# Two transposes of a graph kernel moved from TensorE to VectorE, with their inputs fetched in blocks

## The chip, the cores and the metric

The kernel runs on one core of one Trainium2 chip. A core has five engines that run their own instruction streams in order: TensorE (PE in the profile; PEld is its weight load), VectorE (DVE), ScalarE (ACT), GpSimd (POOL) and SyncE (SP), which here only issues DMAs. Engines wait for each other, and for DMAs, on semaphores. The metric is the device time of one launch in microseconds.

## What is computed

64 graphs, each with 256 nodes and 256 features, in float32. Layer 0 is a normalised graph convolution with residual and layer norm, layer 1 a long convolution over nodes and a message pass, whose results go through a GRU cell, again with residual and layer norm.

```python
# layer 0
deg = adjacency_matrix.sum(axis=-1)
deg = jnp.where(deg != 0, deg, 1.0)
d_inv_sqrt = deg ** (-0.5)
norm_adj = d_inv_sqrt[:, :, None] * adjacency_matrix * d_inv_sqrt[:, None, :]
a_plus = norm_adj + alpha_eff * jnp.eye(N, dtype=adjacency_matrix.dtype)
h = jnp.einsum('bnm,bmf->bnf', a_plus, x)
x = _layernorm(x + jnp.einsum('bnf,pf->bnp', h, W) + b, axis=-1)
# layer 1
xc = jnp.transpose(x, (0, 2, 1))
h = jax.nn.relu(_bn(_conv1d(xc, conv1_w, 0), ...))
h = _bn(_conv1d(h, conv2_w, 8), ...)                 # 17 taps
x_conv = jnp.transpose(jax.nn.relu(h + xc), (0, 2, 1))
s = x @ w_se.T + b_se
dist = sq[:, :, None] + sq[:, None, :] - 2.0 * jnp.einsum('bnd,bmd->bnm', s, s)
A = jnp.exp(-dist) * mask                            # mask is adj
msg = jax.nn.relu(x @ w_msg.T + b_msg)
x_nmp = jnp.einsum('bnm,bmd->bnd', A, msg)
x_in = jnp.concatenate([x_conv, x_nmp], axis=-1)
# GRU cell of (x_in, x), then residual and layer norm
x = _layernorm(x + gru(x_in, x), axis=-1)
```

## The kernel before

[...] the kernel needs adj and the layer 0 result x1 in two layouts: as they lie in memory (nodes on partitions) and transposed.

**Stages.** The 64 graphs are split into four parts q of 16. The convolution with 17 taps is done in the frequency domain, over a whole part at a time. First comes a setup stage (about 30 to 300 us): graphs 0 to 15 go through layers 0 and 1, and beside them `weights()` turns the taps into frequency weights (p_u on TensorE, copies u_set on ScalarE, a VectorE and a GpSimd pass, and three stores of 480 KB a part to the DRAM tensor ud, issued by GpSimd). Then, for each part q: the frequency products of that part (p_k, twelve steps, loading ud again), their inverse, and the GRU gates (p_rz and p_n) of its 16 graphs, with the two layers of the next 16 graphs beside them. The last part has no following graphs.

**One graph.** `layer0(g)` (lines 337 to 411): loads adj_t and x_t (L99, L101; two buffers each, issued by SP three graphs ahead); degrees on ScalarE by an accumulating copy whose main output goes to a part of adjT that is written later (L347); dis = deg^-0.5 on GpSimd (L360); four TensorE transposes of adj into a PSUM bank (L369) and a ScalarE copy into adjT (L370); the diagonal on VectorE (L372); x scaled by dis into x1 on ScalarE (L382); x_t + b on GpSimd (L383). It then yields. The second piece is p_hT (L390) and its ScalarE copy hT (L395), the third p_out (L400), the residual on VectorE (L405), the layer norm (VectorE L311 to L313 and L322, GpSimd L314, ScalarE L324) and the store of x1 to DRAM (L410), issued from ScalarE's queue. x1 has two buffers.

`x1_transposed(g)` (L413 to L420) is four TensorE transposes of x1 (L419) and a ScalarE copy (L420) into xn, the transposed input of layer 1.

`layer1(g)` (L422 to L510): p_conv (L434), bias on VectorE (L437) and relu on ScalarE (L438) give h; p_msg (L455) gives msg; p_dft (L471) takes h to the frequency domain; p_rows (L484) and p_dist (L495) give the distances, the exponential (L496) and the multiply by adjT (L497) give aT; p_nmp (L504) and its copy (L508) end it, with the store of xn (L509).

**Order.** Each function is a generator. `graphs()` walks over layer1(g) and, after each of its pieces, takes a piece of layer0(g+2) or of the other work, as the tuple PLACES says:

```python
PLACES = (("other",), ("layer0",), (), (), ("layer0",), ("other", "layer0"), ())
```

This is the order in which instructions are recorded. The order on each engine is made from it at build time by a list scheduler, which orders what is ready by estimated times; `tc.issue_after(op)` forces an instruction behind another. At run time each engine follows its list in order, so an instruction that waits holds all those behind it. Tiles come from rotating pools: a tile with `bufs=1` is written again only when all readers of its last content are done, a DMA that stores it among them.

Of the kernel before, what the change touches and what calls it, by code (L numbers as in the profile page):

```python
# [9 lines left out]
F32 = mybir.dt.float32  # L10
# [4 lines left out]
P = 128  # L15
# [11 lines left out]
def kernel(  # L27
# [27 lines left out]
    nc = tc.nc  # L55
# [7 lines left out]

    FL, NT = 48, 32
    GT = N // NT
    Q = P // GT
    NQ = B // Q
    assert N == 256 and D == 256 and B % Q == 0 and TAPS == FL - NT + 1 and FL == 3 * NT // 2
# [23 lines left out]

    xin, ain = {}, {}

    def load(g):
        if g >= B:
            return
        ain[g] = loads.tile([P, NCH, N], F32, name="adj_t")
        nc.sync.dma_start(ain[g], adj[g].rearrange("(c p) m -> p c m", p=P))  # L99
        xin[g] = loads.tile([P, NCH, D], F32, name="x_t")  # L100
        nc.sync.dma_start(xin[g], x[g].rearrange("(c p) f -> p c f", p=P))  # L101

# [9 lines left out]
    vectors = const.tile([16, P], F32, name="bn_in")  # L112
    neg_half = const.tile([P, 4], F32)
    nc.vector.memset(neg_half, -0.5)
    load(0)
    nc.scalar.dma_start(alpha_t, bcast_rows(alpha, 1))

    nc.scalar.copy(bc1[:, :4], neg_half)
    for i, a in enumerate((bn1_g, bn2_g, bn1_b, bn2_b, bn1_m, bn2_m, bn1_v, bn2_v)):
        (nc.sync if i % 2 else nc.scalar).dma_start(vectors[2 * i : 2 * i + 2], a.rearrange("(c p) -> c p", p=P))  # L120
    nc.scalar.dma_start(w0, w0T.rearrange("(k p) o -> p k o", p=P))
    load(1)
    nc.sync.dma_start(b0_t, bcast_rows(b0, D))
    nc.sync.dma_start(wc1[:, :, :D], conv1T.rearrange("(k p) o -> p k o", p=P))
    nc.sync.dma_start(wc1[:, :, D:], w_seT.rearrange("(k p) o -> p k o", p=P))
# [204 lines left out]
    x1_d = [dram.tile([Q, N, D], F32, name=f"x1_d{q}") for q in range(NQ)]  # L330
    xn_d = [dram.tile([P, 2 * DCH, N], F32, name=f"xn_d{g}") for g in range(B)]
    XN = {}
    ALONE = set()
    ADJT, X1, X_SCALED, DIAGONAL = {}, {}, {}, {}


    def layer0(g):

        a_t, x_t = ain.pop(g), xin.pop(g)

        adjT = work.tile([P, NCH, 3, P], F32, name="adjT", bufs=3)
        ADJT[g] = adjT

        deg = small.tile([P, NCH], F32, name="deg")
        def degrees():
            for c in range(NCH):
                nc.scalar.activation(  # L347
                    adjT[:, c, 0:2, :].rearrange("p n q -> p (n q)"), a_t[:, c, :], AF.Copy,
                    accum_out=deg[:, c : c + 1],
                )  # L350

        if g == 1:

            with tc.issue_after(X_SCALED[0]):
                degrees()
        else:
            degrees()
        nc.vector.scalar_tensor_tensor(deg, deg, 0.0, deg, op0=ALU.is_equal, op1=ALU.add)  # L358
        dis = small.tile([P, NCH], F32, name="dis")
        nc.gpsimd.tensor_tensor(dis, deg, neg_half[:, :NCH], op=ALU.pow)  # L360
        adeg = small.tile([P, NCH], F32, name="adeg")
        nc.vector.tensor_scalar(adeg, deg, alpha_t, None, op0=ALU.mult)

        p = bank("p_adjT").rearrange("p (c n) -> p c n", c=NCH)
        for mc in range(NCH):
            for c in range(NCH):
                nc.tensor.transpose(p[:, mc, c * P : (c + 1) * P], a_t[:, c, mc * P : (mc + 1) * P], ident)  # L369
        copied = nc.scalar.copy(adjT[:, :, 0:3:2, :], p.rearrange("p c (n q) -> p c n q", q=P))  # L370
        for mc in range(NCH):
            DIAGONAL[g] = nc.vector.scalar_tensor_tensor(  # L372
                adjT[:, mc, 1, :], ident, adeg[:, mc : mc + 1], adjT[:, mc, 2 * mc, :],
                op0=ALU.mult, op1=ALU.add,
            ).ins


        x1 = work.tile([P, NCH, D], F32, name="x1")
        X1[g] = x1
        with tc.issue_after(copied.ins) if g < 2 else ExitStack():  # L380
            for c in range(NCH):
                X_SCALED[g] = nc.scalar.activation(x1[:, c, :], x_t[:, c, :], AF.Copy, scale=dis[:, c : c + 1]).ins  # L382
        nc.gpsimd.tensor_tensor(x_t, x_t, b0_t.unsqueeze(1).to_broadcast([P, NCH, D]), op=ALU.add)  # L383

        yield
        hT = work.tile([P, DCH, N], F32, name="hT", bufs=1)
        p = bank("p_hT").rearrange("p (k n) -> p k n", k=DCH)
        for k in range(DCH):
            for mc in range(NCH):
                nc.tensor.matmul(  # L390
                    p[:, k, :], x1[:, mc, k * P : (k + 1) * P],
                    adjT[:, mc, 1 - mc : 3 - mc, :].rearrange("p n q -> p (n q)"),
                    start=mc == 0, stop=mc == NCH - 1,
                )
        nc.scalar.copy(hT, p)  # L395
        yield
        p = bank("p_out0").rearrange("p (c o) -> p c o", c=NCH)
        for c in range(NCH):
            for k in range(DCH):
                nc.tensor.matmul(  # L400
                    p[:, c, :], hT[:, k, c * P : (c + 1) * P], w0[:, k, :], start=k == 0, stop=k == DCH - 1
                )
        for c in range(NCH):
            mark(
                nc.vector.scalar_tensor_tensor(  # L405
                    x1[:, c, :], p[:, c, :], dis[:, c : c + 1], x_t[:, c, :], op0=ALU.mult, op1=ALU.add
                )
            )
        layernorm(x1, nc.scalar)
        nc.scalar.dma_start(x1_d[g // Q][g % Q].rearrange("(c p) d -> p c d", p=P), x1)  # L410
        yield

    def x1_transposed(g):  # L413
        x1 = X1.pop(g)
        xn = XN[g] = work.tile([P, 2 * DCH, N], F32, name="xn")
        p = bank("p_x1T").rearrange("p (k n) -> p k n", k=DCH)
        for k in range(DCH):
            for c in range(NCH):
                nc.tensor.transpose(p[:, k, c * P : (c + 1) * P], x1[:, c, k * P : (k + 1) * P], ident)  # L419
        nc.scalar.copy(xn[:, :DCH], p)  # L420

    def layer1(g, place):  # L422
# [3 lines left out]
        xn, adjT = XN.pop(g), ADJT.pop(g)  # L426
        x1T = xn[:, :DCH]
        yield

        h = work.tile([P, NCH, D + NSE], F32, name="h", bufs=1)  # L430
        for c in range(NCH):
# [60 lines left out]
        for c in range(NCH):  # L492
# [2 lines left out]
            nc.tensor.matmul(p, dl[rows, c * P : (c + 1) * P], dr[rows, :], start=True, stop=True)  # L495
            nc.scalar.activation(aT[:, c].rearrange("p n q -> p (n q)"), p, AF.Exp, bias=nsq[:, c : c + 1], scale=2.0)  # L496
        mark(nc.vector.tensor_mul(aT, aT, adjT[:, :, 0:3:2, :]))  # L497
        yield
        if g in ALONE:
            x1_transposed(g + 1)  # L500
        p = bank("p_nmp").rearrange("p (k n) -> p k n", k=DCH)
        for k in range(DCH):
            for mc in range(NCH):
# [418 lines left out]
    def graphs(first, part, others):  # L922


        for i in part:
            load(first + i + 3)
            given = {"layer0": layer0(first + i + 2) if first + i + 2 < B else iter(()), "other": others[i]}
            for piece, _ in enumerate(layer1(first + i, i)):
                yield
                for name in PLACES[piece]:  # L930
                    if next(given[name], "end") != "end":
                        yield
            yield from given["other"]

    with tc.tile_pool(name="setup", bufs=1) as setup:
        load_taps(setup, 0)
# [1 line left out]
        nc.sync.dma_start(bmsg_t, bcast_rows(b_msg, D))  # L938
        firsts = merge(layer0(0), layer0(1))
        run(take(firsts, 2))  # L940
        load(2)
        tables(setup)
        run(firsts)
        scale2 = next(batch_norms(setup))

        def gate_weights():
            for b, half_inputs, cols in ((B11, 0, 0), (T1, 0, 1), (B21, 1, 0), (B22, 1, 1)):
# [71 lines left out]
    for q in range(NQ):  # L1019
        first = (q + 1) * Q  # L1020
        more = q + 1 < NQ
        end = chain(complex_end(q), copies(V2) if more else iter(()))
        if more:
            if q:
                others = [take(late, 3 if i % 3 == 0 else 2) for i in range(AHEAD)]
            else:
                others = [nothing() for _ in range(AHEAD)]
                ALONE.update(range(first, first + AHEAD))
            TILES[0] = V2
            begin = graphs(first, range(AHEAD), others)  # L1030
        sums(0)
        real = real_transform()
        for step in range(STEPS):
            if step < 4:
                run(products(step))
            else:
                run(merge(products(step), take(real, 1)))
                run(complex_begin(step))
            if q:
                run(take(late, (0, 1, 1, 1, 1, 1, 2, 1, 2, 1, 2, 1)[step] if more else step % 2))  # L1040
            else:
                run(take(begin, 3))
        run(real)
        if not q:
            run(paced(begin, end, RATES[q]))
        elif more:
            run(paced(chain(merge(take(late, 20), take(begin, 6), 3), begin), end, RATES[q]))
        else:
            run(paced(late, end, RATES[q]))
            run(end)  # L1050
        if more:
            run(late)
            run(end)
            if q == 0:
                scope.close()
                gate = ctx.enter_context(tc.tile_pool(name="gate", bufs=2))
            early = gates(q, range(EARLY))
            others = [take(early, 5 if q == 0 else 2) for _ in range(Q)]
            run(graphs(first, range(AHEAD, Q), others))
            run(early)  # L1060
            if q == 0:
                scope, AHEAD, V2 = open_ahead(6)
                ctx.enter_context(scope)
            late = gates(q, range(EARLY, Q))
        else:
            run(gates(q, range(Q)))


# [51 lines left out]
```

## Time and profile before

| what | value |
| --- | --- |
| median of 3 runs | 2164.66 us (2161.34 to 2165.57) |
| profiled execution: time, span | 2162.39 us, 2160.6 us |
| granted TensorE clock | 0.993 |
| DMA, mean over the span | 305.65 MB, 251182 packets, 141 GB/s |
| DMA queue of SP's and ScalarE's loads, q1 | 183530 packets, 30.0% of 16 engines |
| DMA queue of stores, q10 | 44480 packets, 8.7% |
| GpSimd's queue, q0 | 23024 packets, 8.5% |
| adj transposes L369 and their copies L370 | 39.8 us on PE, 37.0 us on ACT (64 copies) |
| x1 transposes L419 and their copies L420 | 39.1 us on PE, 37.6 us on ACT (64 copies) |

The durations are those of one profiled execution, whose span is 1.8 us shorter than its device time. Busy times are sums of instruction durations. Matmuls are pipelined, so that a listed TensorE duration may be longer than the time after which the next one starts. A shape is written as partitions x elements per partition. "[1.93 <-DVE ln_mr L322]" after a line of the timeline means that the engine stood idle 1.93 us before it and that VectorE's writing of ln_mr released it.

### The profile page before, as it was taken

Reading aid. Unit: us, or ns where it says so; the run is one execution under the profiler, and the core shown is the slowest. Engines: PE = TensorE matmul, PEld = TensorE weight load, DVE = VectorE, ACT = ScalarE, POOL = GpSimd, SP = SyncE. Lnnn points to the kernel's source line nnn. Section 1 sums busy time; section 2 is a strip of 40 time slices with the busy share of each in tenths; the row PEclk is TensorE's granted clock in tenths of the full one; section 3 lists DMA queues with packets and bytes.
Section 4 is the critical chain, followed back from the end, with each engine's and each line's share of the span. In section 5 each row is a group of like instructions: output and inputs, shape, how many; then the busy total and the mean of one; then the engine's idle time right before and its main releaser. Section 6 shows DMA issues by size and latency. Waiting matters only on the chain.

```text
span 2160.6 us, 29043 instructions
## 1 busy us (share of the span) xinstructions
PE 2058.4 (95%) x9805; PEld 1745.5 (81%) x9805; DVE 1547.2 (72%) x3691; ACT 834.7 (39%) x1857; POOL 665.5 (31%) x640
## 2 busy tenths in 40 slices
PE   7999999887999999899999999999999998999998
PEld 5888788776788888788888888778888887788887
DVE  5555577775568788775556988876556889977776
ACT  4665643456331123455443122446543122222222
POOL 2444310122431244223222133323231124444442
PEclk9999999999999999999999999999999999999999
DMA  4766666434347644243336654325334834444441
GB/s 122 236 193 199 194 197 209 144 123 153 87 123 228 195 110 135 98 132 113 108 94 189 201 165 112 118 99 153 92 97 134 249 113 120 126 123 103 113 107 54
DMA packets 251182, 305.65 MB, mean 141 GB/s; under 512 B 18174, under 2 KB 229714, under 8 KB 251034
## 3 DMA queue, kind: packets, MB, share of 16 engines
q1 hardware_dynamic: 183530, 200.46, 30.0%
q10 hardware_dynamic: 44480, 67.39, 8.7%
q0 software_dynamic: 23024, 35.95, 8.5%
q8 instruction: 78, 1.28, 0.2%
q14 instruction: 70, 0.57, 0.1%
HBM read 200.62 MB, written 103.06 MB: 141 GB/s over the span
## 4 chain that ended last, share of the span: by engine, by line
PE 45%; DVE 13%; issue 8%; POOL 6%; ACT 4%; DMA 1%; ACTq 0%; POOLq 0%; DVEq 0%
PE p_rz L808 17%; PE p_n L845 8%; PE p_k L530 7%; PE p_out L400 2%; PE p_nmp L504 2%; PE p_hT L390 2%; POOL ln_rs L314 1%; PE p_dft L471 1%; PE p_conv L434 1%; POOL xc_g L765 1%; POOL sums L788 1%; POOL sums L787 1%; PE p_msg L455 1%; PE p_dist L495 1%; ACT inputs L778 1%
## 5 line engine op out<-in xcount | busy, mean ns | idle before, releaser
L845 PE MATMUL p_n<-wn,inputs 128*128 128x256 f32 x1536 | 350.0, 381 | 14.8 <-DVE first L821 14.7
L808 PE MATMUL p_rz<-wrz,sums 128*128 128x256 f32 x1536 | 350.9, 381 | 3.3 <-POOL sums L787 2.4
L845 PEld LDWEIGHTS p_n<-wn,inputs 128*128 128x128 f32 x1536 | 285.8, 190 | 59.7 <-DVE first L821 17.9
L808 PEld LDWEIGHTS p_rz<-wrz,sums 128*128 128x128 f32 x1536 | 290.8, 191 | 48.1 <-issue 5.6
L808 PE MATMUL p_rz<-wrz,inputs 128*128 128x256 f32 x1152 | 271.9, 379 | 0.2
L314 POOL TENSOR_TENSOR ln_rs<-ln_rs,neg_half 128x2 f32<-128x2 f32 x129 | 100.5, 779 | 519.3 <-DVE ln_rs L313 448.0
L808 PEld LDWEIGHTS p_rz<-wrz,inputs 128*128 128x128 f32 x1152 | 217.5, 190 | 30.7 <-issue 1.0
L857 ACT ACTIVATE nn<-gn 128x256 f32<-128x256 f32 x128 | 53.2, 416 | 329.8 <-DVE gn L854 329.5
L530 PE MATMUL p_k<-u,VM 128*128 128x256 f32 x736 | 174.5, 380 | 1.6 <-DVE VM L573 0.9
L787 POOL TENSOR_TENSOR sums<-inputs 128x384 f32<-128x384 f32 x64 | 71.1, 1112 | 332.6 <-ACT inputs L778 299.8
L360 POOL TENSOR_TENSOR dis<-deg,neg_half 128x2 f32<-128x2 f32 x64 | 46.0, 718 | 401.6 <-DVE deg L358 389.6
L324 ACT ACTIVATE x_g<-x_g,ln_mr,ln_rs 128x256 f32<-128x256 f32 x128 | 70.0, 593 | 245.9 <-DVE ln_mr L322 245.9
L530 PEld LDWEIGHTS p_k<-u,VM 128*128 128x128 f32 x736 | 138.3, 190 | 22.5 <-DMA u<-ud 2.0
L471 PE MATMUL p_dft<-fwd,h 128*128 128x240 f32 x512 | 119.8, 378 | 27.8 <-ACT h L438 26.7
L390 PE MATMUL p_hT<-adjT,x 128*128 128x256 f32 x512 | 127.9, 392 | 14.4 <-DVE adjT L372 7.7
L471 PEld LDWEIGHTS p_dft<-fwd,h 128*128 128x128 f32 x512 | 95.4, 192 | 48.4 <-ACT h L438 41.6
L434 PE MATMUL p_conv<-wc,xn 128*128 128x259 f32 x512 | 125.8, 388 | 4.9 <-ACT xn L420 4.9
L383 POOL TENSOR_TENSOR x_t<-x_t,b_t 128x512 f32<-128x512 f32 x64 | 86.5, 1352 | 140.6 <-ACT x L382 88.6
L497 DVE TENSOR_TENSOR aT<-aT,adjT 128x512 f32<-128x512 f32 x64 | 44.3, 692 | 113.5 <-ACT aT L496 113.5
L400 PE MATMUL p_out<-w,hT 128*128 128x256 f32 x512 | 123.1, 383 | 1.4 <-ACT hT L395 0.7
L455 PE MATMUL p_msg<-wmsg,xn 128*128 128x256 f32 x512 | 121.5, 380 | 0.0
L504 PE MATMUL p_nmp<-aT,msg 128*128 128x256 f32 x512 | 121.1, 379 | 0.2 <-DVE aT L497 0.2
(154 smaller groups left out, 3898.6 us busy)
## 6 DMA issues: line engine op xcount, KB each, us to landing
u<-ud SPq DMA_DIRECT2D x284, 256.0 KB
xn_d<-xn ACTq DMA_DIRECT2D x64, 512.0 KB
inputs<-xn_d SPq DMA_DIRECT2D x64, 512.0 KB
ud<-u_set POOLq DMA_DIRECT2D x39, 480.0 KB, 6.0
adj_t<-in_adj_dram SPq DMA_DIRECT2D x64, 256.0 KB
x_t<-in_x_dram SPq DMA_DIRECT2D x64, 256.0 KB
x_d<-x ACTq DMA_DIRECT2D x64, 256.0 KB
xc_d<-VM SPq DMA_DIRECT2D x64, 256.0 KB
```

What stands on the lines that cost most here:

```text
L314: nc.gpsimd.tensor_tensor(rs[:, : len(chunks)], rs[:, : len(chunks)], neg_half[:, : len(chunks)], op=ALU.pow)
L383: nc.gpsimd.tensor_tensor(x_t, x_t, b0_t.unsqueeze(1).to_broadcast([P, NCH, D]), op=ALU.add)
L390: nc.tensor.matmul(p[:, k, :], x1[:, mc, k * P : (k + 1) * P], adjT[:, mc, 1 - mc : 3 - mc, :].rearrange("p n q -> p (n q)"), start=mc == ...
L400: nc.tensor.matmul(p[:, c, :], hT[:, k, c * P : (c + 1) * P], w0[:, k, :], start=k == 0, stop=k == DCH - 1)
L434: nc.tensor.matmul(p, x1T[:, k, c * P : (c + 1) * P], wc1[:, k, :], start=k == 0, stop=k == DCH - 1)
L455: nc.tensor.matmul(p[:, c, :], x1T[:, k, c * P : (c + 1) * P], wmsg[:, k, :], start=k == 0, stop=k == DCH - 1)
L471: nc.tensor.matmul(p[:, t0 * FL : t1 * FL], h[:, c, k * P : (k + 1) * P], fwd[:, first : first + t1 - t0, :].rearrange("p t f -> p (t f)") ...
L504: nc.tensor.matmul(p[:, k, :], msg[:, mc, k * P : (k + 1) * P], aT[:, mc].rearrange("p n q -> p (n q)"), start=mc == 0, stop=mc == NCH - 1,)
L530: nc.tensor.matmul(p[:, j * D : (j + 1) * D], v[:, k, :], u[:, k, :], start=k == 0, stop=k == DCH - 1)
L787: nc.gpsimd.tensor_tensor(S[:, 0], A21, A22, op=ALU.add)
L808: nc.tensor.matmul(p[:, j * D : (j + 1) * D], a[:, k], wrz[:, b, k], start=k == 0, stop=k == HALF - 1)
L845: nc.tensor.matmul(p[:, o * D : (o + 1) * D], lhsT, w, start=j == 0, stop=j == len(part) - 1)
```

## The change

VectorE's `transpose` turns each 32x32 block of a tile by itself. To get a full transpose, the blocks must already lie in their transposed places; this is done by the DMA that fetches the tile: `fetch_blocks` reads a 256x256 matrix from DRAM in four transfers of 32 partitions with 16 runs of 32 floats each.

- adj of graphs 2 to 63 is fetched twice: row by row (adj_t, for the degrees) and in blocks (adj_blocks). Both use the two buffers of one tag. VectorE transposes adj_blocks into adjT.
- x1 of graphs 1 to 63 is fetched in blocks from x1_d, to which layer 0 stores it (L410 before, L449 after), and VectorE transposes it into xn. The fetch is recorded after the first piece of layer1(g−1), the transpose right after the multiply of aT and adj in layer1(g−1).
- `behind(op)` puts every later recorded VectorE instruction after the transpose in VectorE's order.
- The first part of layer 0 (degrees, transpose, dis, diagonal) becomes a piece of its own, which `graphs()` runs at the end of the graph before, a graph ahead; the load of adj is issued after the second piece of layer1, that of x in front.
- The x1 tile has one buffer in place of two; x1_blocks has one.
- ALONE, which let some graphs transpose x1 earlier, is gone.

In the changed file the scaling of x is L421, the store of x1 L449, the residual L444, the layer norm's last step L345, the degrees L374, u_set's copy L317, relu of h L487, p_dft L520.

```diff
+    def fetch_blocks(blocks, y):
+        for b in range(NB):
+            nc.sync.dma_start(
+                blocks[b * RB : (b + 1) * RB], y.rearrange("(s r) (k b j) -> b r k s j", r=RB, k=DCH, j=RB)[b]
+            )
+
+    def load_adj(g):
+        if g >= B:
+            return
+        a_t, a_b = loads.tile([P, NCH, N], F32, name="adj_t", tag="adj"), None
+        nc.sync.dma_start(a_t, adj[g].rearrange("(c p) m -> p c m", p=P))
+        if g > 1:
+            a_b = loads.tile([P, DCH, N // RB, RB], F32, name="adj_blocks", tag="adj")
+            fetch_blocks(a_b, adj[g])
+        ain[g] = a_t, a_b
...
+    def behind(op):
+        order.close()
+        order.enter_context(tc.issue_after(op.ins))
...
     def layer0(g):
-        def degrees():
-            for c in range(NCH):
-                nc.scalar.activation(
-                    adjT[:, c, 0:2, :].rearrange("p n q -> p (n q)"), a_t[:, c, :], AF.Copy,
-                    accum_out=deg[:, c : c + 1],
...
+        else:
+            for c in range(NCH):
+                degrees(c, a_t[:, c, :])
+            behind(
+                nc.vector.transpose(
+                    adjT[:, :, 0:3:2, :].rearrange("p k n (s r) -> p k n s r", r=RB),
+                    a_b.rearrange("p k (n s) j -> p k n s j", n=NCH),
                 )
+            )
...
-        p = bank("p_adjT").rearrange("p (c n) -> p c n", c=NCH)
-        for mc in range(NCH):
-            for c in range(NCH):
-                nc.tensor.transpose(p[:, mc, c * P : (c + 1) * P], a_t[:, c, mc * P : (mc + 1) * P], ident)
-        copied = nc.scalar.copy(adjT[:, :, 0:3:2, :], p.rearrange("p c (n q) -> p c n q", q=P))
+        if g < 2:
...
+        if g > 1:
+            yield
+        x_t = xin.pop(g)
-        x1 = work.tile([P, NCH, D], F32, name="x1")
+        x1 = work.tile([P, NCH, D], F32, name="x1", bufs=1, tag="x1" if g else "x1_blocks")
...
+    def fetched(g):
+        XB[g] = work.tile([P, DCH, N // RB, RB], F32, name="x1_blocks", bufs=1)
+        fetch_blocks(XB[g], x1_d[g // Q][g % Q])
+
     def x1_transposed(g):
...
+        if g:
+            behind(nc.vector.transpose(xn[:, :DCH].rearrange("p k (s r) -> p k s r", r=RB), XB.pop(g)))
+            return
...
     def layer1(g, place):
...
         yield
+        if g + 1 < B:
+            fetched(g + 1)
...
         mark(nc.vector.tensor_mul(aT, aT, adjT[:, :, 0:3:2, :]))
-        yield
-        if g in ALONE:
+        if g + 1 < B:
             x1_transposed(g + 1)
+        yield
...
     def graphs(first, part, others):
-            load(first + i + 3)
-            given = {"layer0": layer0(first + i + 2) if first + i + 2 < B else iter(()), "other": others[i]}
-            for piece, _ in enumerate(layer1(first + i, i)):
+            g = first + i
+            load_x(g + 3)
+            given = {"layer0": ZERO.pop(g + 2, iter(())), "other": others[i]}
+            for piece, _ in enumerate(layer1(g, i)):
                 yield
+                if piece == 1:
+                    load_adj(g + 3)
                 for name in PLACES[piece]:
                     if next(given[name], "end") != "end":
                         yield
-            yield from given["other"]
+            if g + 3 < B:
+                ZERO[g + 3] = layer0(g + 3)
+                next(ZERO[g + 3])
+                yield
+            yield from others[i]
```

## The prediction

> **What bounds the kernel now.** I read the engine shares and the chain that ended last first, then the busy time stage by stage, then the order of events inside one graph of the first stage, and last the DMA engines in single microseconds.
>
> The page:
>
> ```profile
> PE 2058.4 (95%) x9805; PEld 1745.5 (81%) x9805; DVE 1547.2 (72%) x3691; ACT 834.7 (39%) x1857; POOL 665.5 (31%) x640
> PE 45%; DVE 13%; issue 8%; POOL 6%; ACT 4%; DMA 1%; ACTq 0%; POOLq 0%; DVEq 0%
> ```
>
> TensorE is the bound over the whole, VectorE second; ScalarE and GpSimd have room. Work taken from TensorE is worth something; work given to VectorE is not free.
>
> Busy time by stretch (length, then PE, PEld, DVE, ACT and POOL busy, granted clock, DMA share, GB/s):
>
> ```profile
> 30.00:252.00 222.00, 217.32 (x1053) 179.27 (x1052) 120.19 (x316) 133.49 (x310) 98.81 (x93) 0.99 0.64 201
> 400.00:526.00 126.00, 104.89 (x500) 83.14 (x498) 91.33 (x289) 74.34 (x166) 26.08 (x26) 0.98 0.37 125
> 912.00:1156.00 244.00, 236.79 (x1153) 198.41 (x1154) 148.27 (x406) 124.01 (x286) 67.36 (x70) 1.00 0.36 109
> ```
>
> By the records of L504 in the same view (8 for each graph), 13 graphs run in the first stretch (setup, with the frequency weights beside them), 7 from 252 to 400, 8 from 400 to 526, 4 to 645, 3+3 at 750–912 and 1262–1427, and 13 each at 912–1156 and 1427–1661 (with gates); none beside the complex products. TensorE is full in the first and third line. In the second it idles 21 us: that stage is a chain of dependences.
>
> What the removed transposes cost (timeline, TensorE):
>
> ```profile
> 1114.44 0.60 PE L419 MATMUL p_x1T<-ident,x 128*128 128x128 f32 x4
> 1114.87 2.76 PE L808 MATMUL p_rz<-wrz,inputs 128*128 128x256 f32 x12
> ```
>
> The next matmuls start 0.43 us later, so four transposes hold TensorE 0.43 us, not the 0.60 listed. In the same way a 256-column matmul record costs 0.216 us (the twelve p_rz records here: next start after 2.59), 1.73 for a group of eight.
>
> One setup graph (timeline, the lines of one layer 0 and one layer 1 picked out):
>
> ```profile
> 111.55 1.89 PE L400 MATMUL p_out<-w,hT 128*128 128x256 f32 x8
> ...
> 118.21 1.09 ACT L324 ACTIVATE x<-x,ln_mr,ln_rs 128x256 f32<-128x256 f32 x2 [1.93 <-DVE ln_mr L322]
> ...
> 119.33 0.37 ACTq L410 DMA_DIRECT2D x_d<-x  x1
> ...
> 120.22 0.63 ACT L438 ACTIVATE h<-h 128x512 f32<-128x512 f32 x1
> ...
> 127.20 1.89 PE L400 MATMUL p_out<-w,hT 128*128 128x256 f32 x8
> ```
>
> The pitch is 127.20−111.55 = 15.65 us. x1 is normalised 7.75 us after p_out (118.21+1.09−111.55), its store to DRAM issued by 119.7 (8.1 us after p_out), and ScalarE goes on at once with relu (L438), which p_dft (L471) waits for, and with the next graph's x scaling (L382), since x1 has two buffers.
>
> When does that store land? The DMA engines from 121 to 122 us and from 124 to 125 (queue: packets, MB, share of 16 engines):
>
> ```profile
> q0 software_dynamic: 82, 0.30, 87.8%
> q10 hardware_dynamic: 28, 0.03, 10.5%
> ...
> q10 hardware_dynamic: 41, 0.04, 10.9%
> ```
>
> Its queue (q10) still moves packets at 125 us, because the 480 KB stores of ud on q0 share the engines: some 5.4 to 5.8 us after issue. In the gates stage the same store, issued at 1142.08, has moved its last packet by about 1145.3, 3.0 to 3.2 us later.
>
> [...]
>
> **The change, part by part.**
>
> TensorE. 62 adj and 63 x1 transposes go: 125 x 0.43 = 54 us, 0.86 us a graph. This is a ceiling, had only where TensorE is the bound.
>
> ScalarE loses 125 copies (578 and 587 ns by their rows), 73 us; it is not the bound.
>
> VectorE gains 125 transposes. The nearest row is L497, an f32 128x512 pass of 692 ns (684 to 694); I take 0.70 us, 125 x 0.70 = 87 us (72% to about 76%). Bounds: 0.55 us (close to ScalarE's 0.59 for such a copy) to 1.4 us (two passes, or blocks written with stride), 69 to 175 us.
>
> DMA. Four transfers per tile, 512 packets of 128 bytes each: 2048 packets. Between 29 and 32 us only small packets move:
>
> ```profile
> q1 hardware_dynamic: 128, 0.01, 3.0%
> ```
>
> 0.030 x 16 x 3 us / 128 = 11 ns each. So 2048 x 11 ns / 16 = 1.4 us of all engines per tile; I take 1.5 to 2, some 3 to 4 us a graph. Upper bound: as long as a 1 KB packet between 122 and 123 us (0.408 x 16 us / 103 = 63 ns), 8 us a tile, which would be more than the setup stage has left (0.36 of 15.65 = 5.6 us). SP gets 500 issues. Row-major adj still comes, for the degrees.
>
> Moved loads. On SP a setup graph now issues four x1 block fetches, adj, four adj block fetches, x_t, then the seven taps loads that p_u needs. The taps thus stand behind x_t's wait for its buffer, which L444 (the old L405) frees about 3 us after p_out; p_u's five come over 7 us after p_out, so I cost this at nothing; uncovered it would be up to 3 us in those graphs. VectorE's x1 transpose follows the aT multiply, which ends about half a microsecond after p_out starts (110.70+0.69 against 111.55, plus 0.7), before p_conv at +5.6: free, and the copy for which p_conv waited 4.9 us in all is gone. Degrees and dis (ScalarE, GpSimd) move ahead of the norm of x1 and have a graph's time: nothing.
>
> The adj part a graph ahead removes the short waits of p_hT for the diagonal:
>
> ```profile
> PE p_hT L390 <- DVE adjT L372: 7.7, 7, 2.1
> ```
>
> They lie between 400 and 526, with about 4 us of its neighbours: 11 us at most.
>
> The added wait. x1 now has one buffer, shared by reading and storing: the next graph's scaling (L421 of the changed file) may start only when the store of the previous x1 (L449) has landed. ScalarE runs in order. In the changed order, L421 follows L449 with nothing between in 12 consecutive setup graphs (layer 0 of graphs 3 to 14), and again in a few others; behind it stand a u_set copy, relu h (L487), msg. So p_dft waits for the store. Before it, TensorE has p_out, p_nmp, p_conv, p_msg and five of eight p_u: 4 x 1.73 + 5 x 0.43 = 9.1 us from p_out's start. From p_dft to the next p_out (p_dft, p_rows, p_hT, p_dist, three p_u, ScalarE's hT copy) I count 5.7 us. With L421 0.91, the u_set copy 0.57 and h 0.63:
> - store in 3.0 us (by the gates stage, counted from issue): landed 10.9, h done 13.0, pitch 18.7, +3.0 us a graph, +36 us for 12;
> - central: the third ud store and adj now fall later and leave it more room than before, but the block fetches join: landed 12.1, h 14.2, pitch 19.9, +4.2, +50 us;
> - as before, 5.8 us: landed 13.6, pitch 21.5, +5.8, +70 us.
>
> The x1 blocks for layer 1 come from a store one period older, so that wait is covered here.
>
> Elsewhere:
> - 252–400, 7 graphs: −6 ceiling, three of them still setup: −5.
> - 400–526: 11 us of waits go, but with at most one ScalarE instruction between store and scaling, p_hT comes some 1.5 us later (12.1 after p_out against 10.6) in eight graphs, +12: net +2 (−8 to +8).
> - 526–645: −2.
> - 912–1156 and 1427–1661, 26 graphs: ceiling 26 x 0.86 = −22. Here nn, h, degrees or msg stand between store and scaling in most graphs, and p_hT comes 14 to 17 us after p_out on TensorE, scaling being done by 13.8. The x1 blocks are stored, fetched (two times 3 us, plus the issue) and there at 17.5 to 18, wanted by VectorE at 18.5. Close: −15 (−23 to +10).
> - 750–912 and 1262–1427: VectorE is busy 84% there and gets 0.7 us twice a graph: −6 with nothing late.
>
> Sum: +50 −5 +2 −2 −15 −6 = +24. On the profiled execution, 2162.4 (span 2160.6 and 1.8 around it), 2186; the median of the three runs is 2.3 higher: 2188 us.
>
> **Rivals.**
> 1. Faster: the store's wait costs little. For it: in the gates stage it lands in 3 us, and moving ud and loads later could shorten it further. [...] with the full ceilings elsewhere (41 us, 4 of them in the chain-bound stage kept) and the 11 us of diagonal waits, 2162 + 24 − 41 − 8 gives 24 − 41 − 8 = −25: 2137 on the profiled basis, 2140 as a median. It decides at a setup loss under about 2.5 us a graph.
> 2. Slower by far: block transfers. If a 128-byte packet takes 25 ns or more, each tile holds all DMA engines over 3 us; setup, at 0.64 already, gets another 6.4 of 15.65 us, fills up, and stores, taps and block tiles come late; VectorE's transposes stand in its order with layer norm and gates behind them, so in the gates stages their 26 graphs each lose 1 to 2 us instead of gaining 0.6. +24 + 15 + 26 x 1.5, less overlaps: about 2235.
> 3. No net difference: a setup loss of +36 against gains of 36: 2165.
>
> **How the numbers follow.** A measurement tells ±0.2%, 4.3 us. Forecast case, 2170 to 2215: 0.57. Rival 1: 0.21. Rival 2: 0.16. Rival 3: 0.06. Slower 0.57 + 0.16 = 0.73, same 0.06, faster 0.21. Range 2145 to 2235: it leaves out half of each outer rival, 0.18 together. The likeliest case's own range is 2170 to 2215.
>
> **What would show it.** ScalarE's L421 waiting for the DMA of x1_d, about 3 to 5 us, in 12 setup graphs; p_dft waiting for h (before: 26.7 us in 21 waits) some 60 us more; the setup stretch longer by about 50 us; two gates graphs in less than the 40.4 us that they take now (ScalarE's L324 at 1100.56 and 1140.96 us); transposes of 0.6 to 0.8 us. Wrong, if setup keeps its pitch (the store lands before ScalarE asks), if SP or VectorE wait for x1 or adj blocks over 1 us a graph, or if the transposes take twice a pass.

## The result and the profile after

The changed kernel takes 2290.8 us (median of four runs, 2290.0 to 2291.9) against 2164.5 us: ratio 1.058, 95% interval 1.0567 to 1.0592. The forecast was 2188 us, with a range of 2145 to 2235. The sign was right; the loss was 126 us where 24 were forecast. The profiled execution has a span of 2288.2 us against 2160.6.

The busy line of the page, and the setup stretch, first before, then after (length, then busy time of PE, PEld, DVE, ACT and POOL, granted clock, DMA share, GB/s):

```profile
PE 2062.0 (90%) x9305; PEld 1733.1 (76%) x9305; DVE 1578.8 (69%) x3816; ACT 775.8 (34%) x1732; POOL 682.6 (30%) x640
```

```profile
30.00:300.00 270.00, 263.53 (x1278) 217.54 (x1278) 151.62 (x398) 158.84 (x370) 106.92 (x102) 0.99 0.63 196
```

```profile
30.00:300.00 270.00, 202.88 (x796) 159.82 (x796) 110.15 (x288) 102.96 (x234) 96.94 (x78) 0.81 0.60 151
```

TensorE has 500 records fewer and is yet busy 3.6 us longer: at a granted clock of 0.81 in setup (0.99 before) its instructions take longer. In this stretch it idles 67 us, where it idled 6.5 before.

The lag behind the kernel before is the difference between the starts of a graph's p_nmp in the two traces. It says where the time went:

| at graph | 0 | 5 | 10 | 15 | 27 | 31 | 35 | 39 | 47 | 48 | 53 | 55 | 63 |
| --- | --- | --- | --- | --- | --- | --- | --- | --- | --- | --- | --- | --- | --- |
| lag, us | −0.5 | 41.3 | 80.4 | 108.4 | 117.0 | 109.3 | 108.5 | 120.6 | 111.6 | 119.5 | 118.8 | 133.2 | 128.1 |

The 16 setup graphs have 108 us of it, 8 us a graph up to graph 10. Most pairs of graphs beside gates gain 1.3 us, but 14 us go at graphs 38 and 39 and again at 54 and 55 (the pair behind each gives 3 us back), and 8 more go between 47 and 48.

One setup graph (timeline; the start, the duration, the engine, then the instruction, with the idle time before it and its releaser):

```profile
144.10 1.89 PE L439 MATMUL p_out<-w,hT 128*128 128x256 f32 x8
...
150.69 1.09 ACT L345 ACTIVATE x<-x,ln_mr,ln_rs 128x256 f32<-128x256 f32 x2 [1.03 <-DVE ln_mr L343]
...
151.81 0.37 ACTq L449 DMA_DIRECT2D x_d<-x  x1
...
152.61 2.85 PE L314 MATMUL p_u<-taps,dft_w 85*120 85x256 f32 x10 [1.41 <-DVE taps L306]
...
158.85 0.91 ACT L421 ACTIVATE x<-x_t,dis 128x256 f32<-128x256 f32 x2 [7.07 <-DMA x_d<-x]
...
160.12 0.63 ACT L487 ACTIVATE h<-h 128x512 f32<-128x512 f32 x1
...
160.81 3.56 PE L520 MATMUL p_dft<-fwd,h 128*128 128x240 f32 x8 [5.34 <-ACT h L487]
...
168.49 1.89 PE L439 MATMUL p_out<-w,hT 128*128 128x256 f32 x8
```

The pitch is 24.39 us (15.65 before). Everything that the forecast named is there: the store of x1 is issued, L421 waits for it, relu (L487) waits behind L421, p_dft behind relu. But here 7.0 us pass from the issue of the store to L421's start (5.9 to 7.8 in the twelve setup graphs, middle 6.1), and p_dft, after 5.3 us of idleness, takes 3.56 us for what took 1.78.

In the views of waits of ScalarE and TensorE from 30 to 400 us (us in total, times, longest) this is

```profile
ACT x L421 <- DMA x_d<-x: 60.5, 11, 7.8
...
ACT x L421 <- DMA taps<-in_conv2T_dram: 25.7, 4, 7.4
```

```profile
PE p_dft L520 <- ACT h L487: 64.8, 15, 6.5
PE p_u L314 <- DVE taps L306: 23.0, 12, 7.4
```

Before, p_dft did not wait there at all, and p_u waited 0.9 us for the taps in the whole execution. (In four graphs the profile names a taps load as what came last for L421, which does not read the taps. In the trace the last taps load of each of these graphs signals the same semaphore as the store (number 109 for the store of 103.83 and the load of 109.81), so the name need not be right.)

The transposes themselves cost what was reckoned (group line: busy, then mean ns):

```profile
L461 DVE STREAM_TRANSPOSE xn<-x_blocks 128x512 f32<-128x512 f32 x63 | 44.4, 705 | 11.7 <-DMA x_blocks<-x_d 9.9 <-DMA xc_g<-xc_d 1.8
```

### The profile page after: what moved, and what is told of

Same layout as the page of the kernel before. It is cut to its first block, busy times and chain, and to the rows that moved or that the text cites. A ratio compares the mean times of both kernels' runs of the same rounds, so it can differ in the third digit from the quotient of the medians.

```text
span 2288.2 us, 28698 instructions
## 1 busy us (share of the span) xinstructions
PE 2062.0 (90%) x9305; PEld 1733.1 (76%) x9305; DVE 1578.8 (69%) x3816; ACT 775.8 (34%) x1732; POOL 682.6 (30%) x640
## 5 line engine op out<-in xcount | busy, mean ns | idle before, releaser
L520 PE MATMUL p_dft<-fwd,h 128*128 128x240 f32 x512 | 148.8, 444 | 118.2 <-ACT h L487 117.7
L520 PEld LDWEIGHTS p_dft<-fwd,h 128*128 128x128 f32 x512 | 112.7, 229 | 150.0 <-ACT h L487 138.6
L537 DVE COPY dist_r<-p_rows 64x256 f32<-64x256 f32 x64 | 27.3, 426 | 208.6 <-ACT dist_l L535 208.1
L345 ACT ACTIVATE x_g<-x_g,ln_mr,ln_rs 128x256 f32<-128x256 f32 x128 | 70.0, 593 | 265.2 <-DVE ln_mr L343 265.2
L429 PE MATMUL p_hT<-adjT,x 128*128 128x256 f32 x512 | 135.1, 411 | 15.9 <-ACT x L421 13.2
L397 POOL TENSOR_TENSOR dis<-deg,neg_half 128x2 f32<-128x2 f32 x64 | 61.6, 963 | 246.7 <-DVE deg L395 245.7
L429 PEld LDWEIGHTS p_hT<-adjT,x 128*128 128x128 f32 x512 | 102.1, 212 | 36.0 <-ACT x L421 17.8
```

The source lines that it names most:

```text
L345: nc.scalar.activation(y[:, c, :], y[:, c, :], AF.Identity, bias=mr[:, c : c + 1], scale=rs[:, c : c + 1])
L429: nc.tensor.matmul(p[:, k, :], x1[:, mc, k * P : (k + 1) * P], adjT[:, mc, 1 - mc : 3 - mc, :].rearrange("p n q -> p (n q)"), start=mc == ...
L520: nc.tensor.matmul(p[:, t0 * FL : t1 * FL], h[:, c, k * P : (k + 1) * P], fwd[:, first : first + t1 - t0, :].rearrange("p t f -> p (t f)") ...
```

## The experiments

Medians beside the kernel before on the same chip (2163.9 to 2167.1 us in these sets); intervals are of the ratio.

| run | us | ratio, 95% interval |
| --- | --- | --- |
| two x1 in setup (e1) | 2239.8 | 1.0323 to 1.0354 |
| scaling behind relu (e2) | 2257.0 | 1.0371 to 1.0429 |
| setup on TensorE (e3) | 2200.8 | 1.0142 to 1.0172 |
| adj alone (e4) | 2202.5 | 1.0143 to 1.0190 |
| two x1, taps early (e6) | 2288.1 | 1.0542 to 1.0573 |
| all on TensorE (e7) | 2189.1 | 1.0090 to 1.0120 |
| taps early (e8) | 2287.1 | 1.0533 to 1.0569 |
| rows of 1 KB (e9) | 2232.5 | 1.0290 to 1.0321 |
| two x1, xn on POOL (e10) | 2240.9 | 1.0305 to 1.0370 |
| two x1, taps early, xn on POOL (e11) | 2204.3 | 1.0162 to 1.0206 |
| xn on POOL (e12) | 2290.2 | 1.0552 to 1.0587 |
| dis late (e13) | 2292.4 | 1.0562 to 1.0599 |
| ud after scaling (e17) | 2258.7 | 1.0417 to 1.0447 |
| graphs 40–47, 56–63 (e14) | 2150.4 | 0.9921 to 0.9946 |
| graphs 36–47, 52–63 (e15) | 2166.7 | 0.9998 to 1.0021 |
| graphs 32–63 (e16) | 2165.9 | 0.9995 to 1.0012 |
| 32–37, 40–47, 56–63 (e18) | 2140.2 | 0.9870 to 0.9903 |
| the same and 50–53 (e19) | 2138.3 | 0.9868 to 0.9898 |

**Is it the wait for the store?** Two x1 buffers for setup:

```diff
-        x1 = work.tile([P, NCH, D], F32, name="x1", bufs=1, tag="x1" if g else "x1_blocks")
+        if g < Q and g % 2:
+            x1 = SETUP[0].tile([P, NCH, D], F32, name="x1")
+        else:
+            x1 = work.tile([P, NCH, D], F32, name="x1", bufs=1, tag="x1" if g else "x1_blocks")
```

> The x1 tiles of odd graphs below 16 lie in a buffer of their own, so that in the setup stage the scaling of x no longer waits for the store of the x1 before it; all else as in the changed kernel. Theory A (the setup stage lost its 108 us to ScalarE standing in order behind that store): a setup graph comes down from 24.4 to 15 to 17 us, the whole to 2180 to 2200. Theory B (the block fetches and the late x_t and taps loads hold the setup stage anyway): taps and x1 blocks take the store's place as what ends last, a graph stays at 20 us or more, the whole above 2240.

51 of the 126 us came back. That is far from theory A and just at the edge of theory B. TensorE's waits from 30 to 400 us show what was left:

```profile
PE p_u L314 <- DVE taps L306: 27.3, 12, 7.6
PE p_dft L523 <- ACT h L490: 14.6, 5, 5.7
```

p_u waits for VectorE's multiply of the taps (L306), as it did for 23.0 us in the changed kernel. This multiply is recorded after the transpose of adj, and `behind` forces it after that transpose in VectorE's order, which itself stands behind the layer norm.

The second form leaves one buffer and moves the scaling:

```diff
-        with tc.issue_after(copied.ins) if g < 2 else ExitStack():
+        with tc.issue_after(copied.ins) if g < 2 else tc.issue_after(RELU[0]) if 2 < g < Q else ExitStack():
...
+        RELU[0] = nc.scalar.activation(h[:, :, :D], h[:, :, :D], AF.Relu).ins
```

> One x1 buffer as in the changed kernel, but in graphs 3 to 15 the scaling of x stands behind relu of h in ScalarE's order. Theory A (what costs is what stands behind the wait): p_dft no longer waits for the store, p_hT does; with 8 us to the store's issue, 7 us of landing and 0.9 us of scaling p_hT comes about 16 us after p_out, and the next p_out at 18.5 to 19.5 us: whole 2225 to 2240. Were the store's landing alone the matter (in no order of ScalarE's could it be hidden), it stays above 2270. Theory B: as for two buffers, 20 us a graph or more.

2257.0: p_hT waits for the scaling (16.2 us in six waits to 400 us), but the taps wait is there too (32.6 us), and a gain of 34 us came where 51 to 66 were expected.

> Graphs below 16 are transposed on TensorE as before the change, with no block fetches, and with two x1 buffers; the other 48 as in the changed kernel. Theory A: as the run with two x1 buffers within 15 us either way, since 16 graphs of block fetches are not what costs: 2175 to 2195. Theory B: this run reaches 2175 to 2190, and the run with two x1 buffers stays 50 us above it.

> Only adj is transposed by VectorE; x1 is transposed on TensorE as before, at the changed kernel's place, with two x1 buffers everywhere and no x1 blocks. Theory A: the wait for the store is gone in every stage, and so are the fetches of x1 blocks; the 62 adj transposes are worth up to 27 us of TensorE: 2140 to 2175, the setup graph at 15 to 16.5 us. Theory B: adj blocks still load the DMA engines (half of the block fetches): above 2200.

Here the block path runs only for `g >= Q` (e3), or for adj alone (e4), with two x1 buffers in setup (e3) and everywhere (e4). They end at 2200.8 and 2202.5, above what theory A allowed (2195 and 2175); e4 lies where theory B put it. The two x1 buffers of e1 stay 39 us above e3, so the block path in setup costs: its fetches, VectorE's transposes and the order forced behind them, which these runs do not separate. Something else may cost in both. The next run takes the order alone, with two x1 buffers:

```diff
-        if g < 2:
+        if g < B:        # TensorE transposes of adj everywhere
...
-        if g:
+        if g >= B:       # the same for x1
```

> Both transposes on TensorE as before in all graphs, two x1 buffers, no block fetches; what stays of the change is the order: adj's part a graph ahead, adj loaded later, x1's transpose right after the multiply of aT and adj. It tells the order's own price from that of VectorE's transposes. Order neutral: 2160 to 2172. If the order itself costs (adj alone on VectorE lost 36 us, TensorE in setup lost 34): 2185 to 2205.

2189.1: the new order loses 23 us with no transpose moved at all, 14.6 of them by graph 15. Which part of the order does it was not separated.

**What is left of setup.** The taps of the next part are scaled at the end of a part, so that they no longer stand behind adj's transpose:

```diff
-        nc.vector.tensor_mul(tp, tp, scale[:KT].unsqueeze(1).to_broadcast([KT, ng, D]))   # start of weights(n)
...
+                if n + 1 < NPARTS:
+                    scaled(n + 1, scale)                                                  # end of weights(n)
```

> Two x1 buffers in setup, and the taps of the next part are scaled by VectorE at the end of a part, so that this multiply no longer stands behind the transpose of adj in VectorE's forced order. Theory C (what two x1 buffers left of the setup loss, some 51 us, is p_u waiting for that multiply, 1.4 to 2.1 us a graph, and TensorE's lower clock after it): the waits of p_u for taps go from 27 to under 5 us, the clock of the setup stage from 0.89 to above 0.96, the graph to 15.2 to 16.2 us: whole 2185 to 2205. Theory B (the block fetches slow the taps and x_t loads themselves): the multiply then waits for its taps' DMA in the same place, and the whole stays above 2225.

> Taps scaled early, but one x1 buffer as in the changed kernel. The order that results has relu of h ahead of the scaling of x, so the wait for the store reaches p_hT and not p_dft. Theory A with C: as the run with scaling behind relu, less the taps part: p_hT about 16 us after p_out, graph 18.5 us, whole 2205 to 2235. If one of the two mechanisms were alone the cause: 2290 (unchanged) or 2190.

Both missed: 2288 and 2287. The taps waits did vanish (0.5 us in e6), and another wait came. SP's view of e6 from 30 to 400 us, then its timeline of one graph:

```profile
SPq L101 <- DMA xn_d<-xn: 130.9, 12, 13.1
```

```profile
132.94 13.63 SPq L101 DMA_DIRECT2D adj_blocks<-in_adj_dram  x4
...
151.31 0.71 DVE L397 STREAM_TRANSPOSE adjT<-adj_blocks 128x512 f32<-128x512 f32 x1 [7.10 <-DMA adj_blocks<-in_adj_dram]
```

The four fetches of one tile stretch over 13.6 us, because the last waits for a store that it has nothing to do with: xn's. In the built program each DMA of SP and ScalarE signals one of eight semaphores in turn, and must wait for the one eight places before it on the same semaphore. The trace of the changed kernel shows it: 186 or 187 of the 1493 such DMAs on each of the eight, and xn's store of 148.37 on semaphore 108, for which the x_t load of 151.12, on 108 too, waited. A setup graph now has 19 such DMAs in place of 11, so the turn comes round twice in it, and an SP load can fall on xn's store of the current graph, which ScalarE issues late; all SP loads behind it wait too. In e6 it hits an adj fetch, so VectorE's transpose waits 7.1 us with h behind it in the forced order. In the changed kernel it hits x_t, with the taps behind it (SP, 30 to 400 us):

```profile
SPq L120 <- DMA xn_d<-xn: 103.2, 11, 12.4
```

The test moves xn's store of graphs below 16 to GpSimd's queue, which has other semaphores (in the changed kernel its 103 DMAs signal eight of their own, 12 or 13 each):

```diff
-        nc.scalar.dma_start(xn_d[g], xn)
+        (nc.gpsimd if g < Q else nc.scalar).dma_start(xn_d[g], xn)
```

> As the run with two x1 buffers and early taps, with the stores of xn of graphs below 16 on GpSimd's queue. Theory D: that run lost 48 us because its fourth adj block fetch, and with it VectorE's transpose and all behind it in VectorE's order, waited for the current graph's xn store (131 us of SP waits, 82 us of VectorE waits for adj blocks); here both are gone and theory C's gain shows: the setup graph 15 to 16.5 us, whole 2180 to 2210. Without theory D it stays above 2260.

> Two x1 buffers in setup, and the stores of xn of graphs below 16 go through GpSimd's queue instead of ScalarE's. Theory D (SP's loads stand in order behind a load that waits for a completion semaphore last used by the current graph's xn store; with eight block fetches more a graph the eight semaphores come round within one graph): in this form no SP load waits for xn's store (68 us of x_t's waits in the run with two x1 buffers), so the taps and blocks come earlier; p_u still waits for the taps' multiply in VectorE's order. Whole 2205 to 2235, against 2240. Without theory D: 2235 to 2245.

> The changed kernel with the stores of xn of graphs below 16 on GpSimd's queue; one x1 buffer. ScalarE's wait for the store of x1 stays, but x_t and so the taps are issued earlier, and their packets no longer share the engines with that store; it should land in 5 to 6 us instead of 7. Theory A: graph 22 to 23.5 us, whole 2265 to 2285. If the store's landing is set by the ud stores alone: 2285 to 2292.

e11 falls from 2288 to 2204, SP no longer waits for xn's store, and the setup lags by only 4.7 us at graph 10 (80 in the changed kernel) and 17.9 at graph 15, where the order alone (e7) has 14.6. e10 missed: without early taps the shift gives nothing (2240.9 against 2239.8); p_u waits 24.4 us for the taps multiply, and now SP's last taps load waits for the x1 store (63.0 us). e12 is unchanged: L421 starts a little sooner after the store's issue (middle 5.8 us in place of 6.1), but the store is issued 0.6 us later. So the three causes cover for each other: one undone gives 51, 4 and 1 us, all three 87. Two reservations: each of these runs also gets another order from the scheduler, and early taps with xn on GpSimd's queue, but one x1 buffer, was not run.

Then the packets. Fetching rows of 1 KB in place of blocks, on e6, so that VectorE transposes blocks in the wrong places (the output is then off by 0.374, relative):

> As the run with two x1 buffers and early taps, but the eight block fetches of a graph read whole rows of 1 KB (64 packets each in place of 512); so VectorE transposes blocks that lie in the wrong places, and adjT and xn hold other values. It prices the 128-byte packets. If they matter: 15 to 40 us less than with blocks, above all in setup (DMA share 0.60 to 0.70 there down to 0.5). If the number of transfers and their waits count and not the packets: within 5 us.

It is 56 us faster, but not for one reason: the scheduler gave another order, and the block fetches hardly wait for xn any more (8.4 us where e6 has 130.9; SP's largest wait is 52.4 us for x1 stores). The price of the packets is not settled by it.

**Why 6 to 8 us for the store.** The DMA engines in the changed kernel from 152 to 153, 153 to 154 and 157 to 158 us (queue: packets, MB, share of 16 engines); q0 carries ud, q10 the store of x1 issued at 151.81:

```profile
q0 software_dynamic: 87, 0.32, 98.2%
...
q10 hardware_dynamic: 8, 0.01, 3.2%
...
q10 hardware_dynamic: 28, 0.03, 8.3%
```

Two ud stores, issued at 148.66, hold 98.2 and 93.6% of the engines from 152 to 154; the x1 packets then share them with SP's loads (q1, 51.2% from 157 to 158). The test takes the ud stores away:

```diff
-                for d, u in zip(ud, (us[0], us[3], us[2])):
-                    nc.gpsimd.dma_start(d[:, n * ng : (n + 1) * ng], u)
+                STORES.append((n, us))
...
-        nc.gpsimd.tensor_tensor(x_t, x_t, b0_t.unsqueeze(1).to_broadcast([P, NCH, D]), op=ALU.add)
+        with tc.issue_after(nc.gpsimd.tensor_tensor(x_t, x_t, b0_t.unsqueeze(1).to_broadcast([P, NCH, D]), op=ALU.add).ins):
+            stores()
```

> The changed kernel, but the three stores of ud of a part are issued by GpSimd only after the scaling of x of the next graph, so none of them shares the DMA engines with the store of x1; ScalarE's order is the same. If the ud stores are what stretches the store of x1 from 3 to 7 us: ScalarE's wait falls from 7 us a graph to about 3.5, the graph from 24.4 to 20 to 21.5, the whole to 2240 to 2265. If the taps loads and the fetches stretch it, or if it takes 7 us by itself: above 2280.

2258.7, as expected for contention with ud: 32 us of the 126. From the store's issue to the scaling that waits for it, 2.4 to 4.7 us pass in the setup graphs (middle 3.0). One of them:

```profile
135.60 0.40 ACTq L460 DMA_DIRECT2D x_d<-x  x1
...
138.82 0.91 ACT L431 ACTIVATE x<-x_t,dis 128x256 f32<-128x256 f32 x2 [3.25 <-DMA x_d<-x]
```

**The stages with gates.** In the changed kernel, between p_nmp of graphs 38 and 39 (timelines of GpSimd, VectorE and TensorE):

```profile
1099.29 1.16 POOL L397 TENSOR_TENSOR dis<-deg,neg_half 128x2 f32<-128x2 f32 x1
...
1100.93 1.12 POOL L335 TENSOR_TENSOR ln_rs<-ln_rs,neg_half 128x2 f32<-128x2 f32 x1
```

```profile
1102.09 0.95 DVE L343 SCALAR_TENSOR_TENSOR ln_mr<-ln_mv,ln_rs 128x2 f32<-128x2 f32 x1 [4.85 <-POOL ln_rs L335]
```

```profile
1104.65 0.69 PE L533 MATMUL p_rows<-ident,scols 128*128 128x128 f32 x2 [4.10 <-DVE scols L496]
```

GpSimd did the gates' sums and dis before the power of the layer norm (ln_rs), VectorE stood before ln_mr with scols behind it, and p_rows waited. Was it dis, now computed a graph ahead?

```diff
-        nc.gpsimd.tensor_tensor(dis, deg, neg_half[:, :NCH], op=ALU.pow)
+        if g < 2:
+            nc.gpsimd.tensor_tensor(dis, deg, neg_half[:, :NCH], op=ALU.pow)
...
         if g > 1:
             yield
+            nc.gpsimd.tensor_tensor(dis, deg, neg_half[:, :NCH], op=ALU.pow)
```

> The changed kernel with only dis (the power on GpSimd) moved back from the part done a graph ahead to the part just before the scaling of x. In the stages with gates, the two graphs after each four (38 and 39, 54 and 55) lost 14 us each time in the changed kernel while GpSimd did sums and dis ahead of the layer norm's power, and VectorE waited for it with the node distances behind. If dis ahead in GpSimd's order is the cause: 10 to 25 us of these 28 come back, and the setup stage moves by under 10 either way. If the gates' sums are: no change there.

The lag still grows from 112.8 to 126.6 over graphs 38 and 39. But this run does not answer the question: dis was recorded later, yet the scheduler left it ahead of ln_rs in GpSimd's order. In e13's timeline:

```profile
1106.42 1.16 POOL L414 TENSOR_TENSOR dis<-deg,neg_half 128x2 f32<-128x2 f32 x1
...
1108.07 1.12 POOL L335 TENSOR_TENSOR ln_rs<-ln_rs,neg_half 128x2 f32<-128x2 f32 x1
...
1109.22 0.95 DVE L343 SCALAR_TENSOR_TENSOR ln_mr<-ln_mv,ln_rs 128x2 f32<-128x2 f32 x1 [4.78 <-POOL ln_rs L335]
```

The last runs put the change into chosen graphs only, on the kernel before, with x1 and x1_blocks taking turns in two buffers:

```diff
+    def new(g):
+        return 40 <= g < 48 or 56 <= g < B        # e14; the other runs differ here alone
```

> The kernel before, with the whole change (blocks, VectorE transposes, adj a graph ahead, forced order) for graphs 40 to 47 and 56 to 63 alone, which in the changed kernel took 1.3 us less for each pair of graphs. If that gain is the transposes' own: 8 pairs, 8 to 12 us less than before, 2152 to 2160. If it is only that loss made just ahead is recovered: 2160 to 2175.

> The same for graphs 36 to 47 and 52 to 63. If the 14 us that graphs 38 and 39, 54 and 55 lost each time come with the change where gates start beside it: 10 to 30 us more than the run with 40 and 56. If they came from stages before: as that run, another 3 us less.

> The same for all graphs from 32 on, so without the setup stage and the second part. The changed kernel's graphs 32 to 63 lost 19 us net (109 to 128). If that loss is theirs: 2178 to 2192. If it needs the first 32 graphs: 2150 to 2170.

> The kernel before with the change for graphs 32 to 37, 40 to 47 and 56 to 63. If the loss belongs to graphs 38 and 39 alone and the gain of 5 to 11 us that the run from 32 on had over its graphs 28 to 37 is real: 2138 to 2150. If leaving and entering the changed order costs as much: 2150 to 2160.

> As the run with 32 to 37, and graphs 50 to 53 too. If those gain as in the run from 32 on (4.6 us from 49 to 52): 2134 to 2148. If not: within 4 us of the run with 32 to 37.

e14 beats both kernels and lies 2 us below the expected 2152 to 2160; e15 gives all of it back, and its lag rises by 11.5 us from graph 37 to 39 and by 13 from 53 to 55. So the loss belongs to those four graphs, beside which GpSimd begins a new set of the gates' sums. e16 ends level with before, not at the 2178 to 2192 expected if the loss were these graphs' own. Its lag falls by 12 us to graph 36, then rises by 11 at graphs 38 and 39, by 9 at 48 and by 16 from 52 to 55. e18 and e19, which leave 38 and 39 (and 54 and 55) alone, reach 2140.2 and 2138.3, 1.2% below the kernel before. Their two intervals overlap; 50 to 53 add nothing that can be told. Of the 23 us by which e18 is ahead at graph 63, 7 come between graphs 27 and 31, whose own transposes are as before; why was not looked into.

The traces allow one comparison of GpSimd's order. Between p_nmp of graphs 38 and 39 the sums stand ahead of ln_rs in the changed kernel, e13, e15 and e16, and this step takes 18.9 to 23.2 us; they stand behind it in the kernel before, e14 and e18, and it takes 14.2 to 15.2. But they stand behind it in e7, e9 and e4 too, where the step takes 16.5, 18.3 and 20.6; and the step from 37 to 38, which has no such sums, also loses 5 us in the changed kernel. So GpSimd's order goes with part of the loss. That it is the cause is not shown.

## Why the forecast was wrong, by its own steps

- **Ceiling of 0.86 us a graph, transposes of 0.70 us, packets.** Right in size. VectorE's transposes took 705 (x1) and 701 ns (adj). Between 161 and 162 us of the changed kernel 995 packets of the block fetch held 79.0% of 16 engines, 12.7 ns each (11 were reckoned). The gain of 1.3 us a pair beside gates is three quarters of the ceiling of 1.72.
- **The added wait: the right mechanism, mis-sized.** The central case had the store landed 12.1 us after p_out and h done at 14.2. In the twelve setup graphs L421 started 13.6 to 15.5 us after p_out (mean 14.2) and h was done at 15.5 to 17.8 (mean 16.3). That is 2.1 us a graph. The reason given for the central value, more room for the store than before, was wrong. Only the third ud store fell later; the two others were issued 3.2 us before the store of x1 in both kernels, and the loads of x_t and the taps now ran beside it. e17 shows the part of the ud stores. (The 24 us of setup loss in rival 1's sum stood for a landing faster than 3.0 us. That was the author's estimate; the shortest time from issue to scaling in e17 is 2.4 us.)
- **"As before, 5.8 us" was taken for the worst case.** It was no bound: in eleven of the twelve setup graphs L421 started later than its 13.6 us. It came from the kernel before, where SP had issued the taps ahead of the store.
- **"From p_dft to the next p_out I count 5.7 us".** Measured 6.8 to 8.4, mean 7.9. The count was right where TensorE did p_dft in 1.89 us: five such setup graphs of e17 took 5.8. That it would run slower after its stall (3.56 us for p_dft, 1.78 before) was in no term; it is 2.2 us a graph. With the 2.1 above it accounts for nearly all of the mean pitch of 24.3 us in place of 19.9, so that setup cost 104 us for the twelve graphs and not 50.
- **"The taps thus stand behind x_t's wait for its buffer ... I cost this at nothing".** Wrong twice. x_t waited for the semaphore of xn's store (103 us), not for its buffer, and the taps multiply had moved behind adj's transpose in VectorE's order. In the changed kernel both lay under the larger wait for the store, since undoing either alone gives 1 and 4 us; e1 and e6 lay them open. Rival 2 had named late taps and blocks, but put them down to slow packets.
- **"Degrees and dis ... move ahead ...: nothing".** The order was given no price. Alone it costs 23 us (e7), of which 14.6 are in setup; how much of this lies under the wait for the store in the changed kernel is not known.
- **252 to 400 us, −5.** Measured +5.6 from graph 15 to 19, which e7's order does not explain (14.6 to 14.7): it stays open.
- **Gates, −15.** Measured +10 (35 to 47: +3.1; 51 to 63: +7.3). Most pairs gained as the forecast said; graphs 38, 39, 54 and 55, which lost 28 us together, were not looked at by themselves. Why they lose stays open.
- **The small terms.** 400 to 526: +3.0 from graph 19 to 27 (+2 forecast). 526 to 645: −7.7 from 27 to 31 (−2). 750 to 912 and 1262 to 1427: −0.8 from 31 to 35 and +9.2 from 47 to 51 (−6 together); 7.9 of these go at graph 48. e16, in which graph 48 is changed too, loses 9.4 there; e14, e15, e18 and e19, in which it is not, lose at most 0.9. The cause was not looked for.

## What to carry to other kernels

A single buffer that is also the source of a store puts the store's landing into the next user's engine (here 5.9 to 7.8 us a setup graph from issue to scaling), and what stands behind that instruction in the engine's order pays; the landing must be taken from the moment at which the store now runs, with what then shares the engines, not from its quietest or its present place. A stall can have a second price on TensorE: here p_dft after it took 3.56 us, where it had taken 1.78. An experiment that moves an instruction has to be checked in its own trace, since the scheduler may put it back where it was (e13). And before a change goes into a whole loop, look where in the loop its price differs: here the change, with its two x1-sized buffers taking turns and limited to graphs that the lag showed to gain, turned +5.8% into −1.2%.

## What the runs showed of the hardware

- After a stall of 5.34 us TensorE did p_dft in 3.56 us instead of 1.78, and the granted clock of the whole setup stretch was 0.81 (0.99 before). In e1, with shorter waits of p_dft (14.6 us to 400 us in place of 64.8), it was 0.89; the whole of e11 had 0.98 (0.96 in the changed kernel). In five setup graphs of e17 the same p_dft took 1.89 us after stalls of 1.3 to 1.9 us, but in another 3.56 us after one of 1.1: the length of the stall just before it does not tell it alone.
- From the issue of the same 256 KB store to the start of what waits for it, 5.9 to 7.8 us passed (middle 6.1) beside two stores of 480 KB on another queue, and 2.4 to 4.7 us (middle 3.0) when those came later (e17).
- VectorE's transpose of a 128x512 float32 tile took 701 to 705 ns, a two-input pass of the same size 693 ns.
